# A four-part transformer block on one Trainium2 core: weight-block preparation placed behind each tile's last sum, priority for some sums, and one normalisation on ScalarE

## The chip, the cores and the metric

The kernel runs on one core of a Trainium2 chip. The metric is the device time of one execution in microseconds (us). The engines are TensorE (PE, with its weight loads shown apart as PEld), VectorE (DVE), ScalarE (ACT), GpSimd (POOL) and SyncE (SP, which issues nearly all of the DMAs here). Each engine works through its own instructions strictly in their order, and waits at the head of its queue for what that instruction needs.

## The reference, cut to what matters

The input is x, 4 batch entries of 512 tokens with 1024 channels each, in float32. Four layers follow one another, each with a layer norm (LN, no weights) ahead of it and a residual around it:

```python
x = x + attn0(LN(x))   # at each position: softmax attention among the 4 batch entries
x = x + ffn0(LN(x))    # h @ W_base.T + b_base + sum over 8 experts of
                       #   rw[e] * (h @ A[e].T) @ B[e].T, rank 16,
                       #   rw = softmax over the two largest of h @ W_gate.T, else 0
x = x + mla(LN(x))     # causal attention, 32 heads, low-rank q and kv, RoPE, output matrix wo
x = x + ffn1(LN(x))    # as ffn0, but rw[e] is one softmax over 8 experts for each batch entry,
                       #   from the mean of its tokens 179 to 510
```

## The kernel before, in words

The 2048 tokens are 16 tiles of 128 tokens, four tiles for each batch entry. A float32 product is done as three products of a reduced type: each operand is split into a high part (a cast, mostly on ACT) and a low part (operand minus high part, on DVE or POOL), and `matmul3` (L131 to L135) adds low x high, high x low and high x high in one PSUM bank. A scheduler lays out each engine's instructions from the program order, their dependencies and priorities. `tc.high_priority()` moves the instructions under it ahead where the data allow it. `tc.issue_after(ins)` puts the instructions under it behind `ins` in the order of an engine. It is an ordering of the schedule and adds no semaphore. Tiles of SBUF and PSUM come from pools with a fixed number of buffers, and a buffer that is taken again waits for its last reader.

**First feed-forward layer (about 107 to 380 us).** The loop over tiles stands at L465, with `s` the place of the tile in the order. The product of a tile has 1160 columns (gate, the experts' A, and base weights) in three parts of 392, 384 and 384, each in a PSUM bank. The pool `b_po` has six banks, so two tiles fit. For tile s, PE does in turn: part 0 of tile s+1; the transpose of tile s's weighted expert activations (`weigh`); part 1 of tile s+1; the transposes of the normalised tile s+2 (`turn0`); part 2 of tile s+1; and the product with the experts' B, into the banks of tile s (`finish`, L324). Then DVE adds each of the three banks to x (L333), which frees the bank; part 0 of tile s+2 needs the first one. Beside that DVE does the router's small steps (`route`), the normalisation (L124), and half of the splits. POOL adds the bias to x (L479). Every fourth tile the statistics of the next four tiles are taken (`statistics`, L119): those that the next layer needs at tiles 3, 7 and 11, and those of this layer at tiles 1, 5 and 9.

**Block preparation.** In the same loop, at tiles 2 to 9, `prepare_w1(room1, s - 2)` (L366 on) prepares eight blocks of weights for the last layer. That layer's matrix product is cut into two by two blocks and done with seven products instead of eight, some of which use differences of weight blocks. For each of the eight, DVE does four subtractions (L372, 128 x 288), ACT four copies (L375), POOL four subtractions (L376), and SP four writes to DRAM (L377, `w_t<-raw`). Then the next block is fetched (L363, `raw<-in_w_dram`). All of it lives in one room of SBUF, of which four parts hold the fetched block and three pairs of parts hold results, taken in turn (`n = 4 + 2 * ((4 * u + n) % 3)`). When the eight blocks are done, the room becomes `rawA`, into which the weights `waT` of the attention are loaded (L498 to L500). After each tile's sums SP writes the tile to DRAM (`x_d`, L492).

**Attention (about 380 to 1560 us).** It isn't touched, but for its end. `project(g, b, behind)` (L824) multiplies the context of a group of eight heads and one batch entry with the output matrix, in the same seven-product form: `b11, t1, t2, b22, t3, b21, t4`, into PSUM banks `poa` and `pob`. After each product DVE adds the bank to a piece `xs` of x (L877). ACT and POOL make the splits `cxh` and `cxl` (L838, L839) of the next operands.

**Transition (about 1555 to 1615 us).** The last `project`, of group NG-1 and batch NB-1, runs interleaved with the start of the second feed-forward layer: `norm(0, t)` (L1077) normalises the two tiles of the first pair from `xo[0]`, where x has been loaded, into `hs[0]`, by one DVE instruction each (L124); `turn1` (L1081) transposes them, four transposes to a PSUM bank, which ACT copies; `operands` (L1098) makes sums and differences s1, s2, s4 (L1103) and splits them. `split_w1` (L988) splits weight blocks `wb` on DVE or POOL.

**Second feed-forward layer (to the end).** Eight pairs of tiles, seven products each (`product`, L1221), for two column halves (`problems` holds the halves). After each, DVE adds the bank to `xo` (L1244). For the first pair the two halves are done one after the other, so there `problems` has one member; for all later pairs it has two.

Of the kernel before, what the change touches and what calls it, by code (L numbers as in the profile page):

```python
# [9 lines left out]
F32 = mybir.dt.float32  # L10
FR = mybir.dt.float32r
AF = mybir.ActivationFunctionType
ALU = mybir.AluOpType
# [4 lines left out]
P = 128  # L18
# [27 lines left out]
def block_kernel(ctx: ExitStack, tc: tile.TileContext, a: dict, out: bass.AP):  # L46
# [277 lines left out]
    def finish(xt, po, hw, cols, bt, to=None):  # L324

        at = 0
        first = cols[-1][1] - D
        for s, (c0, c1) in enumerate(cols):
            skip = first if s == 0 else 0
            n = c1 - c0 - skip  # L330
            matmul3(po[s][:, skip : c1 - c0], hw[0], hw[1], bt[0][:, at : at + n],
                    bt[1][:, at : at + n], start=False, stop=True, skip_group_check=True)
            V.tensor_tensor(xt[:, at : at + n], xt[:, at : at + n], po[s][:, skip : c1 - c0],  # L333
                            ALU.add)
            if to is not None:
                nc.sync.dma_start(out=to[:, at : at + n], in_=xt[:, at : at + n])
            at += n

    LAST = slice(2, 3)

# [25 lines left out]
    def prepare_w1(room, u):  # L366

        c, s = divmod(u, 2)
        b11, b12, b21, b22 = (room[:, k * W1B : (k + 1) * W1B] for k in range(4))
        for n, (kind, to, a0, a1) in enumerate((("t1", b11, b12, b11), ("t3", b12, b22, b12),  # L370
                                                ("t2", b22, b22, b11), ("t4", b21, b21, b22))):
            V.tensor_tensor(to, a0, a1, ALU.subtract)  # L372
            n = 4 + 2 * ((4 * u + n) % 3)
            h, l = (room[:, (n + k) * W1B : (n + k + 1) * W1B].bitcast(FR) for k in range(2))
            A.copy(h, to)  # L375
            G.tensor_tensor(l, to, f32(h), ALU.subtract)  # L376
            nc.sync.dma_start(  # L377
                out=w1_d[kind, s][:, :, c, :],
                in_=room[:, n * W1B : (n + 2) * W1B].rearrange("p (k n) -> p k n", k=2))
        if u + 1 < ND:  # L380
            fetch_w1(room, u + 1)
# [18 lines left out]
    with tc.tile_pool(name="b_h", bufs=2) as hp, tc.tile_pool(name="b_hTh", bufs=2) as hTh, \  # L400
            tc.tile_pool(name="b_hTl", bufs=2) as hTl, tc.tile_pool(name="b_w", bufs=1) as bwp, \
            tc.tile_pool(name="b_work", bufs=2) as wk, \
            tc.tile_pool(name="b_pt", bufs=2, space=PSUM) as ptp, \
            tc.tile_pool(name="b_po", bufs=6, space=PSUM) as pop:
        with tc.tile_pool(name="b_stB", bufs=1) as stage:
            b0h, b0l = load_split(bwp, stage, a["b0T"], [P, D], "b0", G)
        bias0 = broadcast_rows(bwp, a["b0"], D, "bias0")

        def route(lg):


            def best(values):
                m = small.tile([P, 1], F32, name="best")
                V.tensor_reduce(m, values, AX.X, ALU.max)
                eq = wk.tile([P, E], F32, name="eq")
                V.scalar_tensor_tensor(out=eq, in0=values, scalar=m, in1=rank,
                                       op0=ALU.is_equal, op1=ALU.mult)
                k = small.tile([P, 1], F32, name="key")
                V.tensor_reduce(k, eq, AX.X, ALU.max)
                one = wk.tile([P, E], F32, name="one")  # L420
                V.tensor_scalar(one, eq, k, None, ALU.is_equal)
                return m, one

            m1, one1 = best(lg)
            rest = wk.tile([P, E], F32, name="rest")
            V.scalar_tensor_tensor(out=rest, in0=one1, scalar=NEG, in1=lg, op0=ALU.mult, op1=ALU.add)
            m2, one2 = best(rest)
            e2 = small.tile([P, 1], F32, name="e2")
            V.tensor_tensor(e2, m2, m1, ALU.subtract)
            A.activation(e2, e2, AF.Exp)  # L430
            w1 = small.tile([P, 1], F32, name="w1")
            V.tensor_scalar(w1, e2, 1.0, None, ALU.add)
            V.reciprocal(w1, w1)
            w2 = small.tile([P, 1], F32, name="w2")
            V.tensor_tensor(w2, e2, w1, ALU.mult)
            rw = wk.tile([P, E], F32, name="rw")
            V.tensor_scalar(rw, one1, w1, None, ALU.mult)
            V.scalar_tensor_tensor(out=rw, in0=one2, scalar=w2, in1=rw, op0=ALU.mult, op1=ALU.add)
            return rw

        def routed(po):
            lg = wk.tile([P, E], F32, name="lg")
            V.tensor_copy(lg, po[0][:, ER : ER + E])
            return route(lg)

        def turn0(s):
            t = order[s]
            h = hp.tile([P, D], F32, name="h")
            with tc.high_priority() if s < 2 else ExitStack():
                normed.append(normalise(h, x[:, t, :], *stats0[s // NB], s % NB))  # L450
            return transposed(h, (hTh, hTl), ptp)

        normed = []
        hts = {0: turn0(0), 1: turn0(1)}
        po = {0: base(hts[0], w0, W0_COLS, pop, slice(0, 3))}
        room1 = raw()
        for kind in ("b11", "b22", "b21"):
            row, col = int(kind[1]) - 1, int(kind[2]) - 1
            for s in range(2):
                nc.sync.dma_start(  # L460
                    out=w1_d[kind, s][:, 0],
                    in_=a["w1"][row * ND // 2 : (row + 1) * ND // 2, :,
                                (2 * s + col) * W1B : (2 * s + col + 1) * W1B].rearrange("c p n -> p c n"))
        fetch_w1(room1, 0)
        for s, t in enumerate(order):  # L465
            if s + 1 < NT:
                po[s + 1] = base(hts[s + 1], w0, W0_COLS, pop, slice(0, 1))
            q, k = divmod(s, NB)
            hw = weigh(po[s], routed(po[s]), ptp, wk) if s + 1 < NT else hw_last
            if s + 1 < NT:  # L470
                po[s + 1] += base(hts[s + 1], w0, W0_COLS, pop, slice(1, 2))
            if k == 1 and q + 1 < TPB:
                with tc.issue_after(normed[1].ins):
                    stats0[q + 1] = statistics([x[:, n * TPB + q + 1, :] for n in range(NB)])
            if s + 2 < NT:
                hts[s + 2] = turn0(s + 2)
            if s == NT - 1:
                hts1[1] = turn1(1, ptp)
            G.tensor_tensor(x[:, t, :], x[:, t, :], bias0, ALU.add)  # L479
            if s == NT - 2:  # L480
                hw_last = weigh(po[s + 1], routed(po[s + 1]), ptp, wk)
            if s + 1 < NT:
                po[s + 1] += base(hts[s + 1], w0, W0_COLS, pop, LAST)
            if s == NT - 2:
                wpools.close()
                hTh1 = c1.enter_context(tc.tile_pool(name="c1_hTh", bufs=2, side="right"))
                hTl1 = c1.enter_context(tc.tile_pool(name="c1_hTl", bufs=2, side="right"))
                hp1 = c1.enter_context(tc.tile_pool(name="c1_h", bufs=2, side="right"))
                hts1[0] = turn1(0, ptp)
            finish(x[:, t, :], po.pop(s), hw, W0_COLS, (b0h, b0l))  # L490
            for k_ in range(2):
                nc.sync.dma_start(out=x_d[t][k_], in_=x[:, t, k_ * 512 : (k_ + 1) * 512])  # L492
            if k == NB - 1 and q < TPB - 1:
                stats1[q] = statistics([x[:, n * TPB + q, :] for n in range(NB)], "c", 4)
            if 0 <= s - 2 < ND:
                prepare_w1(room1, s - 2)
            if s == ND + 2:
                rawA = raw()  # L498
                for ch in range(ND):
                    nc.sync.dma_start(out=rawA[:, ch * NA : (ch + 1) * NA], in_=a["waT"][ch])  # L500
                split_shared(firstp, 0)
# [210 lines left out]
    with ExitStack() as c2:  # L712
# [111 lines left out]
        def project(g, b, behind):  # L824
# [17 lines left out]
            for j in range(0, TPB, 2):  # L842
# [16 lines left out]
                for kind, bank, start, to, last in (  # L859
# [11 lines left out]
                    for c, (wh, wl) in enumerate(w[kind]):  # L871
# [2 lines left out]
                                skip_group_check=True)  # L874
                        if c + 1 < HG // 4:
                            yield
                    V.tensor_tensor(xs[to], xs[to], banks[bank], ALU.add)  # L877
                    if last and (g, b) == (NG - 1, 0):
                        V.bn_stats(stats_d[j + to[0]][:, to[1], :], xs[to])
                    if last:  # L880
# [195 lines left out]

        def norm(q, t):  # L1077
            s = 2 * q + t
            normalise(hs[q][t], hs[q][t] if q else xo[0][t], *stats[s][0], stats[s][1])

        def turn1(q, half):  # L1081

# [138 lines left out]
    def product(q, step, problems):  # L1221
# [5 lines left out]
        for s in problems:  # L1227
# [13 lines left out]
                else:  # L1241
                    V.tensor_tensor(to, to, ps[:, 0:ER], ALU.add)
            to = xo[q][t][:, at : at + W1B - skip]
            V.tensor_tensor(to, to, ps[:, skip:W1B], ALU.add)  # L1244
            if kind == "t4" and q % 2:
                at = slice(0, 2 * W1B - ER) if s == 0 else slice(2 * W1B - ER, D)
                nc.sync.dma_start(out=out_v[:, 2 * q + 1, at], in_=xo[q][1][:, at])
# [124 lines left out]
```

## Time and profile before

| | us |
|---|---|
| median of the runs (3) | 1855.22 |
| lowest and highest | 1845.07 and 1857.25 |
| the profiled execution: its own time | 1851.48 |
| its span, first to last instruction | 1849.7 |
| mean TensorE clock granted in the span | 0.982 |

The profile is of one execution; the span lies within that execution's own time. The groups of the first feed-forward layer that matter here, as the profile gives them for the stretch from 107 to 380 us: the 48 sums L333 take 504 ns each (22.8 us); the 32 subtractions L372 take 688 ns each (22.0 us), and DVE stood idle for 12.2 us ahead of them, 11.2 of these for the DMA that fetches the block; the 32 copies L375 take 433 ns each on ACT, and the 32 subtractions L376 take 880 ns each on POOL; the 16 bias sums L479 take 2431 ns each on POOL; the 15 normalisations L124 take 975 ns each on DVE.

A group's line gives the line of code, the engine, the operation, output and input names with their shapes, the number of instructions, the busy time and mean duration, and then how long the engine had stood idle just before these instructions and what ended the idle time. Idle time costs something only on an engine that others wait for.

### The profile page before, as it was taken

The page shows a single profiled execution, that of the slowest core. Times are in us where ns is not written, and L with a number is a line of the kernel's source. Part 1 is how long each engine was busy: PE and PEld are TensorE (multiplying, and loading weights), DVE is VectorE, ACT ScalarE, POOL GpSimd, SP SyncE. Part 2 cuts the span into 40 slices and gives each one's busy share as a digit, 9 for nine tenths or more (in the row PEclk, how much of TensorE's full clock was granted, in tenths as well). Part 3 has the DMA queues.
Part 4 walks back from the last instruction along what each step waited for, and adds up shares of the span by engine and source line. Part 5 has one row for each costly group of instructions (what it writes and reads, how often), then busy time and mean ns, then how long its engine had stood idle before and what let it go on. Part 6 is the DMA issues. An engine that isn't in the chain of part 4 may idle for free.

```text
span 1849.7 us, 30780 instructions
## 1 busy us (share of the span) xinstructions
PE 1744.4 (94%) x10280; PEld 1463.2 (79%) x10280; DVE 1363.8 (74%) x3534; ACT 878.0 (47%) x2272; POOL 915.7 (50%) x819
## 2 busy tenths in 40 slices
PE   6978999999899999999999999999999999779998
PEld 6977899999667777767777767777766777679998
DVE  6787666576697777678777678777678877667785
ACT  6332211156675555466555465555466655323222
POOL 0364211020565566556566556566556665565552
PEclk9989899999899999999999999999999999989999
DMA  7235300035442333353243353242344233643431
GB/s 259 79 121 193 133 35 35 35 93 159 129 142 76 106 131 112 105 169 114 94 137 101 117 170 112 95 142 89 129 150 151 93 133 131 236 155 100 136 116 46
DMA packets 130239, 224.68 MB, mean 121 GB/s; under 512 B 22113, under 2 KB 57953, under 8 KB 127009
## 3 DMA queue, kind: packets, MB, share of 16 engines
q1 hardware_dynamic: 130080, 222.72, 35.9%
q8 instruction: 81, 1.33, 0.3%
q14 instruction: 78, 0.63, 0.1%
HBM read 155.55 MB, written 70.65 MB: 122 GB/s over the span
## 4 chain that ended last, share of the span: by engine, by line
PE 70%; DVE 10%; POOL 4%; ACT 3%; issue 2%; DMA 1%; SPq 0%; POOLq 0%; ACTq 0%; DVEq 0%
PE psv L817 8%; PE pst L801 6%; PE pss L133 3%; PE pss L134 3%; PE pss L135 3%; PE pob L133 3%; PE poa L133 3%; PE po L133 3%; PE po L134 3%; PE po L135 3%; PE psq L133 3%; PE acc L135 3%; PE acc L133 2%; PE pob L134 2%; PE psq L135 2%; PE pob L135 2%
## 5 line engine op out<-in xcount | busy, mean ns | idle before, releaser
L780 ACT ACTIVATE p<-p,mn 128x512 f32<-128x512 f32 (+3 forms) x512 | 284.3, 557 | 236.7 <-DVE mn L777 235.6
L602 POOL TENSOR_TENSOR qf<-qf,ropeT 64x512 f32<-64x512 f32 x128 | 167.7, 1311 | 220.8 <-ACT qf L598 217.1
L777 DVE CUSTOM_DVE_ANT_0 p<-pss,causal 128x512 f32<-128x512 f32 (+3 forms) x512 | 232.0, 487 | 24.8 <-PE pss L135 21.0
L801 PE MATMUL pst<-ident,p 128*128 128x128 f32 x1280 | 186.7, 276 | 5.6 <-ACT pT L803 4.7
L603 POOL TENSOR_TENSOR qf<-qf,t 64x512 f32<-64x512 f32 x128 | 165.6, 1294 | 46.6 <-DVE t L601 39.2
L801 PEld LDWEIGHTS pst<-ident,p 128*128 128x128 f32 x1280 | 154.8, 143 | 31.8 <-ACT pT L803 6.4
L803 ACT COPY pT<-pst 128x512 f32<-128x512 f32 x256 | 143.3, 578 | 58.2 <-PE pst L801 58.2
L133 PE MATMUL pss<-kT,ql 128*128 128x512 f32 (+2 forms) x384 | 144.4, 376 | 19.8 <-DVE mn L777 14.4
L611 POOL TENSOR_TENSOR ql<-qf,qh 128x384 fp32r<-128x384 f32 x128 | 131.3, 1026 | 58.6 <-DVE qh L610 58.6
L839 POOL TENSOR_TENSOR cxl<-s,cxh 128x256 fp32r<-128x256 f32 x128 | 96.7, 756 | 116.9 <-ACT cxh L838 111.6
L133 PE MATMUL po<-w_h,hTl 128*128 128x384 f32 (+1 forms) x384 | 136.0, 354 | 13.4 <-DVE x L333 13.4
L134 PE MATMUL po<-w_l,hTh 128*128 128x384 f32 (+1 forms) x384 | 132.9, 346 | 0.0
L135 PE MATMUL po<-w_h,hTh 128*128 128x384 f32 (+1 forms) x384 | 132.6, 345 | 0.0
L135 PE MATMUL pss<-kT,qh 128*128 128x512 f32 (+2 forms) x384 | 131.1, 341 | 0.0
L134 PE MATMUL pss<-kT,qh 128*128 128x512 f32 (+2 forms) x384 | 131.1, 341 | 0.0
L803 DVE COPY pT<-pst 128x256 f32<-128x256 f32 x128 | 53.8, 420 | 76.3 <-PE pst L801 75.0
L133 PEld LDWEIGHTS pss<-kT,ql 128*128 128x128 f32 x384 | 72.6, 189 | 46.5 <-DVE mn L777 22.8
L598 ACT COPY qf<-psq 128x512 f32<-128x512 f32 x126 | 73.6, 584 | 65.5 <-PE psq L135 65.3
L600 DVE TENSOR_TENSOR t<-psq,ropeT 32x512 f32<-32x512 f32 x126 | 87.7, 696 | 17.2 <-ACT qf L598 13.0
L780 ACT ACTIVATION_READ_ACCUMULATOR p<-p,mn 128x1 f32 x512 | 96.3, 188 | 0.0
L479 POOL TENSOR_TENSOR x<-x,bias 128x1024 f32<-128x1024 f32 x16 | 38.9, 2431 | 106.1 <-DVE h L124 82.3
L601 DVE TENSOR_TENSOR t<-psq,ropeT 32x512 f32<-32x512 f32 x126 | 87.1, 691 | 1.7
(548 smaller groups left out, 5082.4 us busy)
## 6 DMA issues: line engine op xcount, KB each, us to landing
xs<-x_d SPq DMA_DIRECT2D x128, 256.0 KB
x_d<-xs SPq DMA_DIRECT2D x128, 256.0 KB
slotC<-in_woT_dram SPq DMA_DIRECT2D x32, 512.0 KB
rb<-r_d SPq DMA_DIRECT2D x128, 128.0 KB
w_t<-raw SPq DMA_DIRECT2D x32, 288.0 KB
x<-in_x_dram SPq DMA_DIRECT2D x16, 512.0 KB
x_d<-x SPq DMA_DIRECT2D x32, 256.0 KB
slotA<-q_d SPq DMA_DIRECT2D x8, 1024.0 KB
```

The costliest lines, as they stand in the source:

```text
L133: T.matmul(ps, lhsT=al, rhs=bh, start=start, stop=False, **kw)
L134: T.matmul(ps, lhsT=ah, rhs=bl, start=False, stop=False, **kw)
L135: T.matmul(ps, lhsT=ah, rhs=bh, start=False, stop=stop, **kw)
L602: G.tensor_tensor(f[mid], f[mid], ropeT[mid, 0, :], ALU.mult)
L603: G.tensor_tensor(f[mid], f[mid], t2[mid], ALU.add)
L611: G.tensor_tensor(l, f[:, P:S], f32(h), ALU.subtract)
L777: V.tensor_tensor_reduce(out=to, in0=ps[:, 0:n], in1=causal[:, S - n : S], scale=1.0, scalar=-NEG, op0=ALU.add, op1=ALU.min, accum_out=mn[ ...
L780: A.activation(to, to, AF.Exp, bias=mn[:, i : i + 1], scale=-1.0, accum_out=rs[:, i : i + 1])
L801: T.transpose(ps[:, w : w + P], p[:, OF[i] + j * P : OF[i] + (j + 1) * P], ident)
L803: copy(pT[:, AT[js[0]] : AT[js[0]] + w], ps[:, 0:w])
L817: T.matmul(ps[n * KVR : (n + 1) * KVR, S - w : S], lhsT=k[:, j, :], rhs=pTs[u + n][:, AT[j] : AT[j] + w], start=(j == 0), stop=(j == TPB - 1))
L839: G.tensor_tensor(l, src, f32(h), ALU.subtract)
```

## The change

It has three parts. First, `finish` returns its last DVE instruction, and the block preparation is emitted under `tc.issue_after(done.ins)`: the DVE instructions of `prepare_w1` are ordered behind the last of the three sums of the tile at which they stand in the program. Second, two kinds of sums are emitted under `tc.high_priority()`: L877 in the last `project`, and L1244 where only one half is computed, that is for the first pair. Third, `norm(0, t)` is done on ACT, as `rstd * x + off`, with `off = -mean * rstd` from a new DVE instruction on 128 x 1; the later pairs stay on DVE.

```diff
@@ finish
-            V.tensor_tensor(xt[:, at : at + n], xt[:, at : at + n], po[s][:, skip : c1 - c0],
-                            ALU.add)
+            done = V.tensor_tensor(xt[:, at : at + n], xt[:, at : at + n],
+                                   po[s][:, skip : c1 - c0], ALU.add)
             if to is not None:
                 nc.sync.dma_start(out=to[:, at : at + n], in_=xt[:, at : at + n])
             at += n
+        return done
@@ the loop over tiles
-            finish(x[:, t, :], po.pop(s), hw, W0_COLS, (b0h, b0l))
+            done = finish(x[:, t, :], po.pop(s), hw, W0_COLS, (b0h, b0l))
             for k_ in range(2):
                 nc.sync.dma_start(out=x_d[t][k_], in_=x[:, t, k_ * 512 : (k_ + 1) * 512])
             if k == NB - 1 and q < TPB - 1:
                 stats1[q] = statistics([x[:, n * TPB + q, :] for n in range(NB)], "c", 4)
             if 0 <= s - 2 < ND:
-                prepare_w1(room1, s - 2)
+                with tc.issue_after(done.ins):
+                    prepare_w1(room1, s - 2)
@@ project
-                    V.tensor_tensor(xs[to], xs[to], banks[bank], ALU.add)
+                    with tc.high_priority() if (g, b) == (NG - 1, NB - 1) else ExitStack():
+                        V.tensor_tensor(xs[to], xs[to], banks[bank], ALU.add)
@@ norm
-            normalise(hs[q][t], hs[q][t] if q else xo[0][t], *stats[s][0], stats[s][1])
+            (mv, rstd), k = stats[s]
+            if q:
+                return normalise(hs[q][t], hs[q][t], mv, rstd, k)
+            off = small.tile([P, 1], F32, name="off")
+            V.scalar_tensor_tensor(out=off, in0=mv[:, k, 0:1], scalar=-1.0, in1=rstd[:, k : k + 1],
+                                   op0=ALU.mult, op1=ALU.mult)
+            A.activation(hs[0][t], xo[0][t], AF.Identity, bias=off, scale=rstd[:, k : k + 1])
@@ product
-            V.tensor_tensor(to, to, ps[:, skip:W1B], ALU.add)
+            with tc.high_priority() if len(problems) == 1 else ExitStack():
+                V.tensor_tensor(to, to, ps[:, skip:W1B], ALU.add)
```

## The prediction

> **What bounds the kernel now.** I read the page first, then the waits by engine, then the time order of single stages. TensorE carries the kernel, and where it stands still the time is lost.
>
> ```profile
> span 1849.7 us, 30780 instructions
> PE 1744.4 (94%) x10280; PEld 1463.2 (79%) x10280; DVE 1363.8 (74%) x3534; ACT 878.0 (47%) x2272; POOL 915.7 (50%) x819
> PE   6978999999899999999999999999999999779998
> PEclk9989899999899999999999999999999999989999
> ```
>
> Each digit is 46.2 us. Dips of PE stand where the change acts: slices 3 and 4 (139 to 231 us, the first feed-forward layer) and slices 34 and 35 (1572 to 1665 us, attention to second feed-forward layer). I asked for PE's waits in the two stages, 100 to 240 and 1560 to 1612 us:
>
> ```profile
> PE po L133 <- DVE x L333: 13.4, 4, 4.5
> ...
> PE pob L133 <- DVE xs L877: 5.3, 3, 2.4
> PE poa L133 <- POOL cxl L839: 1.2, 1, 1.2
> PE poa L133 <- DVE xs L877: 0.6, 1, 0.6
> ```
>
> Both times PE waits for a sum on DVE that frees a PSUM bank. Busy times by stretches, cut where the first-part products of tiles 2, 3, 4 ... start, show what one tile of the first layer costs (PE busy, PEld, DVE, ACT, POOL, then PE clock, DMA share, GB/s):
>
> ```profile
> 143.74:147.45 3.71, 0.00 (x1) 0.00 (x1) 3.61 (x6) 0.74 (x2) 3.71 (x3) 1.00 0.22 80
> 147.45:166.70 19.25, 16.86 (x91) 16.47 (x91) 14.03 (x36) 4.81 (x13) 9.11 (x10) 0.91 0.65 212
> 166.70:186.50 19.80, 15.30 (x91) 14.90 (x91) 13.91 (x35) 4.47 (x12) 8.62 (x9) 0.98 0.58 192
> 186.50:204.31 17.81, 17.81 (x91) 17.75 (x91) 11.47 (x33) 3.55 (x10) 7.51 (x8) 0.83 0.53 180
> 204.31:222.31 18.00, 15.19 (x91) 14.80 (x90) 14.79 (x48) 5.00 (x9) 3.54 (x3) 1.00 0.41 133
> 222.31:238.99 16.68, 16.68 (x90) 16.61 (x91) 8.20 (x28) 1.55 (x4) 2.40 (x1) 0.90 0.09 32
> 238.99:254.02 15.03, 15.03 (x91) 14.95 (x91) 8.07 (x28) 1.55 (x4) 2.40 (x1) 1.00 0.10 36
> 269.06:284.09 15.03, 15.03 (x91) 14.80 (x90) 14.63 (x47) 3.31 (x7) 2.40 (x1) 1.00 0.10 37
> ```
>
> A tile without block preparation takes 15.03 us, all PE. The stretch from 143.74 to 238.99 us is five tiles: 95.25 us against 75.15, an excess of 20.1 us. Of it 13.4 is standing and 6.7 is slow clock afterwards. The cause, in DVE's time order and on the chain that ended last:
>
> ```profile
> 144.47 2.59 DVE L372 TENSOR_TENSOR raw<-raw 128x288 f32<-128x288 f32 x2
> 174.59 0.46 DVE L372 TENSOR_TENSOR raw<-raw 128x288 f32<-128x288 f32 x1 [2.46 <-DMA raw<-in_w_dram]
> ...
> 169.99 5.20 DMA raw<-in_w_dram
> 181.00 3.57 DMA raw<-in_w_dram
> ```
>
> The 32 preparation subtractions (L372) stand in DVE's queue ahead of the tile sums, and some wait there for their DMA, with the sums behind them.
>
> **What the Trainium skill says.** "TensorE: Matmul & The Clock Gate", What's actually happening: PE falls to half clock after an idle window of about 3.4 us that runs freely, and needs about as long to recover. The trace agrees in kind: gaps of 3.71, 4.50 and 2.81 us were followed by 1.8, 2.8 and 1.65 us of loss, that of 2.39 us by 0.2. "SBUF — State Buffer", Who interferes with whom: a DVE instruction with two SBUF inputs and a GpSimd one that reads SBUF exclude each other for the whole instruction. The trace agrees: L435, a 128x1 product, took 2.19 us beside POOL's 2.40 us bias sum. "ScalarE: Activation LUTs", What ACT_TABLE_LOAD costs: an ACTIVATE is 186 ns, plus 93 ns for each pointer operand, plus 0.833 ns an element; by this estimate the new normalisation is 1.23 us. The trace shows a 128x1024 cast on ACT at 1.05 us.
>
> **Part 1, the ordering edge.** How the instructions stand in both builds shows that it takes hold: the 32 subtractions move from tiles 0 to 4 to behind the sums of tiles 2 to 9, four to a tile. PE's order in this stage is unchanged.
>
> Removed: the excess of 20.1 us, since no L372 is left ahead of the first two sums and the later ones start after their sum. At tile 0, DVE still has the logits, the next tile's normalisation and two splits, all without the DMA waits, so the sum at 143.1 us can follow its product at once.
>
> Added: four subtractions (0.43 to 0.69 us, the least and the mean of the 32) per tile, 1.7 to 2.75 us, and 4 x 0.81 us of POOL work that can block DVE. In a light tile DVE is busy for 8.07 of 15.03 us; it idles 2.31 us before the next logits, 1.53 before the normalisation and 2.52 before the sum. So six light tiles hide it: cost nothing; without that cover 2 us each.
>
> Two of the eight are heavy, tiles 3 and 7, where the next four tiles' statistics come too. There DVE is busy for 14.63 us and the bank is freed just in time (the next product starts 0.2 us late). Four subtractions lengthen it by 1.7 to 2.75 us plus up to 1 us of exclusion by POOL: a gap of 1.5 to 4, taken 2.7, and slow clock of 0.2 to 2.8, taken 1.3. Twice 4.0 is 8.0 us. Part 1: 20.1 - 8.0 = 12.1 us gained.
>
> Its DMAs: the fetch of the next block is issued after POOL's last split, some 6 us into the tile, takes 3.5 to 5.2 us, and is wanted at 15. On SP, the x_d writes now stand ahead of the w_t writes; nobody waits for either. The fourth ACT copy waits for the tile's first w_t write, since three room slots serve four blocks: subtraction 1.2, copy 1.7, POOL 2.55, issue 3.1, landing (2.47 us in the chain) 5.6 us after the product starts. Behind it on ACT stands the router's exponential, whose input comes at 6.4: no cost. The room is free later, about 290 us, so the waT load moves from 207 to 290; its parts are wanted at 372.
>
> **Part 2, priority, and part 3, ACT.** In the transition PE stands:
>
> ```profile
> 1577.09 0.47 PE L133 MATMUL pob<-t10h,cxl 128*128 128x512 f32 x1 [2.45 <-DVE xs L877]
> 1586.53 0.50 PE L133 MATMUL pob<-b220h,cxl 128*128 128x512 f32 x1 [2.09 <-DVE xs L877]
> 1588.82 0.47 PE L133 MATMUL poa<-t30h,cxl 128*128 128x512 f32 x1 [0.62 <-DVE xs L877]
> 1594.12 0.47 PE L133 MATMUL pob<-b110h,cxl 128*128 128x512 f32 x1 [0.79 <-DVE xs L877]
> 1597.10 0.47 PE L133 MATMUL poa<-t10h,cxl 128*128 128x512 f32 x1 [1.23 <-POOL cxl L839]
> ```
>
> That is 7.2 us, plus about 1.6 of slow clock (8 products at 0.43 instead of 0.23 us): 8.8. In the new order sums L877 precede the L1103 combinations and the L988 split, two 0.8 us normalisations leave DVE (two 0.15 us offsets come), and ten of the twelve b11 products of the next layer move behind, where they fill waits. What is late next: POOL's 3.2 us L988 split, now later because its ACT copy stands behind the two ACT normalisations, holds back the split of s1, so t10 starts near 1575.7 instead of 1577.1, 1.5 us after PE is free. Then about 0.5 at t20, 0.7 at b22, and near b21 up to 1.5 us, as DVE's next normalisation now stands behind h loads that are issued after the x_d writes. I take 3.5 us: gain 5.3, bounds 0 and 8. Later, at 1642 us, the s1 combination (2.86 us, blocked by POOL) now stands behind the router's small steps instead of ahead of them; PE stood 3.8 us there, I take 0.8 back (bounds -1 and 2). The chain b11, ah, al, s1, s2, s4, sum that costs 3.23 us at 1612.69 is untouched.
>
> **Sum.** 12.1 + 5.3 + 0.8 = 18.2 us. Profiled execution 1851.48 us (span 1849.7 and 1.8 around it), after: 1833.3. The median of the runs shown is 1855.22, 3.7 more: 1837.0.
>
> **The rivals.**
> - A, the heavy tiles don't stall: new order puts the small steps elsewhere and idle bits take the subtractions. For it: 0.4 us of DVE idle in tile 7; against: DVE at 96% there. Saves 18.5 in part 1 and 6.5 after: 1830.
> - B, the transition gives nothing, because POOL's L988 and the late h loads replace the sums as the last wait. For it: DMA share 0.95 at 1568 to 1577 us; against: 5.9 of 7.2 us wait for L877. Then 1855.2 - 9.2 = 1846.
> - C, slower: the fourth ACT copy waits for the w_t write and holds up exponential, router and sum in each of eight tiles. It decides once the landing takes over 7 us (0.8 us to the exponential, 4 us of DVE idle). Each such tile costs 3 us of standing and 1.7 of clock: 37.6 against 20.1 saved, less 6 in the transition: 1866. Against it: landings of 2.47 us in a DMA share of 0.5, and the share falls to about 0.25.
> - That the edge does nothing is excluded by the order.
>
> **How the numbers follow.** Forecast 0.50 (own range 1832 to 1842), A 0.26, B 0.19, C 0.05. The range of 1826 to 1849 takes in A, B and the bounds. A measurement can tell about 1% of this kernel, 18.6 us, from no change: faster by over 1% is below 1836.7, that is A and two fifths of the forecast, 0.46; within 1% is the rest of the forecast, B and half of C, 0.51; slower 0.03.
>
> **What would show it.** Right: no PE wait on x L333 before the sum of tile 3, tiles of 15.0 us, and two waits of 1.5 to 4 us near tiles 4 and 8; PE waits on xs L877 nearly gone at 1555 to 1590 us. Wrong: PE waiting on L333 in every prepared tile (C), ACT copies of L375 waiting long for w_t, or sums in the transition standing behind a normalisation that waits for its h load (B).

## The result, and the profile after

The changed kernel takes 1836.47 us (median of 11 runs, 1834.84 to 1840.72) against 1849.08 us for the kernel before (median of 11 runs, 1845.06 to 1857.25). The ratio is 0.9933, 95% interval 0.9916 to 0.995: 0.67% or 12.4 us faster, with bounds of 9 and 16 us. The three runs shown ahead of the prediction had a median of 1855.22 us; with eight more the median came out 6 us lower.

The page of the kernel after, the lines that answer to those shown of before:

```profile
span 1834.7 us, 30780 instructions
PE 1741.2 (95%) x10280; PEld 1461.5 (80%) x10280; DVE 1350.6 (74%) x3534; ACT 880.0 (48%) x2274; POOL 917.0 (50%) x819
PE   6979999999899999999999999999999999879998
PEclk9989999999999999999999999999999999989999
```

The dip of slices 3 and 4 is gone, that of slices 34 and 35 is smaller. PE does the same work (1741.2 against 1744.4 us), and the span is 15.0 us shorter. The waits of PE from 100 to 300 us, one line of the answer (sum, times, longest):

```profile
PE po L133 <- DVE x L333: 4.3, 2, 2.1
```

Four waits of 13.4 us became two of 4.3. The stretches, cut at the first products of tiles 4, 5, 6, 7 and 9, 10, 11 (PE, PEld, DVE, ACT, POOL busy, PE clock, DMA share, GB/s):

```profile
173.64:188.74 15.10, 15.10 (x91) 15.02 (x91) 10.27 (x32) 3.28 (x8) 6.26 (x5) 1.00 0.47 153
188.74:206.14 17.40, 15.26 (x91) 14.86 (x90) 17.19 (x52) 6.12 (x12) 6.08 (x5) 1.00 0.39 133
206.14:221.35 15.21, 15.21 (x91) 15.14 (x92) 10.40 (x32) 3.28 (x8) 6.21 (x5) 1.00 0.47 152
251.55:268.95 17.40, 15.26 (x91) 14.86 (x91) 17.19 (x52) 6.12 (x12) 6.08 (x5) 1.00 0.39 133
268.95:285.68 16.73, 16.73 (x90) 16.66 (x91) 10.40 (x32) 3.17 (x8) 6.19 (x5) 0.90 0.42 138
```

A tile with a preparation and no statistics (the first row) costs PE nothing: DVE has 10.27 us of work in 15.10. In the two stretches that hold a preparation and the statistics DVE has 17.19 us of work and the next tile's bank comes 2.14 us late: the late sums are those of tiles 4 and 8, and PE stands ahead of the first products of tiles 6 and 10. Inside the first of them, from DVE's and POOL's order of time:

```profile
193.74 0.95 DVE L373 TENSOR_TENSOR raw<-raw 128x288 f32<-128x288 f32 x1
202.65 2.37 POOL L480 TENSOR_TENSOR x<-x,bias 128x1024 f32<-128x1024 f32 x1 [5.94 <-DVE w L433]
202.87 2.17 DVE L436 TENSOR_TENSOR w<-e,w 128x1 f32<-128x1 f32 x1
205.68 1.34 DVE L333 TENSOR_TENSOR x<-x,po 128x256 f32<-128x256 f32 x3
```

A product of 128x1 took 2.17 us beside a bias sum on POOL; elsewhere it takes 0.16 (that the bias sum is the reason is shown by e9 below). The sums start only after it, with no idle time ahead of them.

The transition, from PE's order of time, the products ahead of which PE stood:

```profile
1563.53 0.50 PE L133 MATMUL pob<-t10h,cxl 128*128 128x512 f32 x1 [0.82 <-POOL cxl L841]
1565.74 0.47 PE L133 MATMUL poa<-t20h,cxl 128*128 128x512 f32 x1 [0.56 <-DVE xs L880]
1568.64 0.47 PE L133 MATMUL pob<-b220h,cxl 128*128 128x512 f32 x1 [0.24 <-DVE xs L880]
1581.61 0.47 PE L133 MATMUL poa<-b220h,cxl 128*128 128x512 f32 x1 [1.64 <-DVE xs L880]
```

Five gaps of 7.2 us became four of 3.3. Of the 7.2 us some 1.3 vary from execution to execution: in e7 and e12 below, where PE, DVE and ACT have the order of the kernel before, the gaps make 5.8 and 5.9 us. Where the 15.0 us of span went can be read by setting each product of one trace against the same product of the other: at the end of the first feed-forward layer the kernel after is 13.4 us ahead, at 1550 us 11.7, behind the last projection 17.8, and from 1660 us on 15.8 to 15.2. So the transition gave 6.1 us with its slow clock, and about 2.2 were lost again at once.

### The profile page after: what moved, and what is told of

It is laid out like the page before. It is cut to its first block, busy times and chain, and to the rows that moved or that the text cites. A ratio compares the mean times of both kernels' runs of the same rounds, so it can differ in the third digit from the quotient of the medians.

```text
span 1834.7 us, 30780 instructions
## 1 busy us (share of the span) xinstructions
PE 1741.2 (95%) x10280; PEld 1461.5 (80%) x10280; DVE 1350.6 (74%) x3534; ACT 880.0 (48%) x2274; POOL 917.0 (50%) x819
## 4 chain that ended last, share of the span: by engine, by line
PE 78%; DVE 10%; POOL 4%; ACT 3%; issue 2%; DMA 1%; SPq 0%; POOLq 0%; ACTq 0%; DVEq 0%
PE psv L819 8%; PE pst L803 6%; PE pss L133 4%; PE po L133 4%; PE po L135 4%; PE po L134 4%; PE pss L134 3%; PE pss L135 3%; PE pob L133 3%; PE poa L133 3%; PE psq L133 3%; PE psq L134 3%; PE psq L135 3%; PE pob L135 3%; PE pob L134 3%; PE acc L135 3%
## 5 line engine op out<-in xcount | busy, mean ns | idle before, releaser
L880 DVE TENSOR_TENSOR xs<-xs,pob 128x512 f32<-128x512 f32 x112 | 76.0, 679 | 15.2 <-PE pob L135 13.5
```

## The experiments

**Each part by itself.** e1 is the kernel before with the edge, e2 with the two priorities, e3 with the normalisation on ACT; each edit is the part of the diff shown above.

> The kernel before with the ordering edge alone. Theory (the gain is DVE's order in the first feed-forward layer): tile starts as in the changed kernel, PE stands for x L333 only twice, about 2.1 us each, ahead of tiles 6 and 10; the last sum of this layer ends about 13.4 us earlier; the transition keeps its five gaps of 7.2 us in all. Time about 13 us below before, ratio 0.993. Rival (most of the gain is made in the transition): ratio 0.996 or above. The changed kernel measured 0.9933, so by the theory nearly all of it is here.

Measured: ratio 0.9929 (0.9908 to 0.995), two PE gaps of 2.19 and 2.21 us ahead of tiles 6 and 10. The last products of the first layer start 16.4 us earlier, 2.0 of which were there before this layer began; the transition has four gaps of 5.95 us, not five of 7.2. The first-layer gain is all there, and with it the whole gain of the change.

> The kernel before with the two priorities alone. The order of instructions shows only two sums moved (the sum at t1 of the second pair of tiles ahead of two operand combinations, and the first sum of the next layer ahead of one); no sum of L1244 after that one moves. Theory (the priority does little): PE gaps on xs L877 fall from 5.9 us to 4 to 6 us, time within 2 us of before, ratio 0.999 to 1.000. Rival (the priority is what shortens the transition): gaps on xs L877 of 1 us or less, 4 to 5 us gained, ratio 0.9975.

Measured: ratio 1.0001 (0.9987 to 1.0016). PE's waits from 1540 to 1610 us:

```profile
PE pob L133 <- DVE xs L878: 4.6, 2, 2.5
PE poa L133 <- DVE xs L878: 1.1, 1, 1.1
```

The waits on the sums are still 5.7 us of 5.9. A priority moves a sum only where the scheduler had something else ahead that could wait; there were two such places.

> The kernel before with the first pair normalised on ACT alone. In the order of instructions this part carries nearly all that moves in the transition and at the mixture. Theory: PE gaps between the last projection's products fall from 7.2 to about 3.4 us, as in the changed kernel, and the wait of PE for the first weighed activations rises from 1.75 to about 3.2 us; together 2 to 4 us gained, ratio 0.998. Rival (the normalisation on ACT costs what it saves): ratio 1.000 or above.

Measured: ratio 0.9999 (0.9986 to 1.0012). The gaps of the transition are those of the changed kernel:

```profile
PE poa L133 <- DVE xs L877: 2.2, 2, 1.6
PE pob L133 <- POOL cxl L839: 0.8, 1, 0.8
PE pob L133 <- DVE xs L877: 0.2, 1, 0.2
```

So the normalisation on ACT, not the priority, made the transition shorter, by 6.1 us in this trace too; and yet the kernel is no faster. Something takes the gain back. One thing was visible in all traces with this part: a light tile of the first layer, more than 1000 us ahead of the changed code, took 15.10 us instead of 15.03 to 15.05.

**The heavy tiles.** e4 is the changed kernel with no preparation where the statistics are:

```diff
+    PREPARE = (1, 2, 4, 5, 6, 8, 9, 10)
...
-            if 0 <= s - 2 < ND:
+            if s in PREPARE:
                 with tc.issue_after(done.ins):
-                    prepare_w1(room1, s - 2)
-            if s == ND + 2:
+                    prepare_w1(room1, PREPARE.index(s))
+            if s == PREPARE[-1] + 1:
```

> The changed kernel, with the eight preparations at tiles 1, 2, 4, 5, 6, 8, 9 and 10 instead of 2 to 9, so none at tiles 3 and 7, and waT loaded one tile later. Theory (four subtractions too many on a DVE that is full in the tiles with statistics): no PE gap above 0.3 us at tiles 2 to 12, all periods about 15.1 us, 4.6 us of standing and up to 1.6 us of slow clock gone against the changed kernel: ratio to before 0.990. Rival (the stall comes from elsewhere in these tiles, for instance the bias sum of POOL that blocks L436 for 2 us): gaps of about 2 us stay and the ratio is 0.993.

Measured: ratio 0.9897 (0.9878 to 0.9916), and no wait on L333 from 120 to 350 us. The stretch of tile 5 in e4:

```profile
190.45:205.65 15.20, 15.20 (x91) 14.86 (x90) 14.86 (x48) 3.31 (x7) 2.41 (x1) 1.00 0.09 35
```

DVE works 14.86 of 15.20 us, and that is just enough, although the 128x1 product still takes 2.21 us there. The other load in these stretches is the bias sum that blocks L436. e6 emits POOL's bias sums of tiles 3 and 7 ahead of `turn0`:

```diff
+            if s in (3, 7):
+                G.tensor_tensor(x[:, t, :], x[:, t, :], bias0, ALU.add)
             if s + 2 < NT:
                 hts[s + 2] = turn0(s + 2)
-            G.tensor_tensor(x[:, t, :], x[:, t, :], bias0, ALU.add)
+            if s not in (3, 7):
+                G.tensor_tensor(x[:, t, :], x[:, t, :], bias0, ALU.add)
```

> The changed kernel, with POOL's bias sum of tiles 3 and 7 emitted ahead of the normalisation of tile s+2, so that it no longer runs beside L436. DVE's order is unchanged. Theory (two things fill DVE in the heavy tiles, the four subtractions and the 2.0 us for which POOL's bias sum blocks L436, and either is enough to close the gap of 2.14 us): L436 takes 0.2 us, the gaps ahead of tiles 6 and 10 fall to below 0.5 us, 4 us gained against the changed kernel, ratio to before 0.991. Rival (the bias sum then blocks other instructions of DVE with two operands in SBUF, above all the subtractions, for as long): gaps of 1.5 us or more stay, ratio 0.993.

Measured: ratio 0.9933 (0.9912 to 0.9953), L436 still 2.17 us, gaps 2.14 and 2.15 us. The edit moved nothing: in the trace every engine has the sequence of operations of the changed kernel, POOL's included. So this run says nothing for or against the bias sum. POOL runs ahead of PE, and the bias sums in the heavy stretches are those of tiles 8 and 12. e9 orders these two behind POOL's splits of a later preparation:

```diff
-            G.tensor_tensor(x[:, t, :], x[:, t, :], bias0, ALU.add)
+            with tc.issue_after(split[s - 6]) if s in (8, 12) else ExitStack():
+                G.tensor_tensor(x[:, t, :], x[:, t, :], bias0, ALU.add)
...
-            G.tensor_tensor(l, to, f32(h), ALU.subtract)
+            split[u] = G.tensor_tensor(l, to, f32(h), ALU.subtract).ins
```

> The changed kernel, with POOL's bias sums of tiles 8 and 12 ordered behind the preparation that follows, which takes them out of the two stretches with statistics (the run before aimed at tiles 3 and 7, whose bias sums do not stand there: POOL runs up to four tiles ahead). DVE's order is unchanged. Theory (in the two heavy stretches DVE is late by the four subtractions and by 2.0 us for which a bias sum blocks L436; the first product there is late by 2.14 us): L436 takes 0.2 us there, the gaps ahead of tiles 6 and 10 fall from 2.14 us to 0.1 to 0.5 us, with the slow clock 4 to 6 us are gained, ratio to before 0.9905. Rival (the subtractions and POOL's splits beside them are the whole of the delay, and DVE idles elsewhere for what it gains): gaps of 1.5 us or more, ratio 0.993.

Measured: ratio 0.9883 (0.9865 to 0.99), a larger gain than expected. Set product against product, the trace of e9 gains 5.5 us on that of the changed kernel in this stage, as expected; the rest arose where the order is the same, and is not explained. The orders of PE, DVE and ACT are those of the changed kernel. The 128x1 product in its order of time, and PE's waits from 120 to 350 us:

```profile
200.87 0.16 DVE L438 TENSOR_TENSOR w<-e,w 128x1 f32<-128x1 f32 x1
```

```profile
PE po L133 <- DVE x L333: 0.2, 1, 0.2
```

The gaps fell from 2.14 to 0.16 and 0.15 us. Two causes added up, and to remove either is enough: e4 took away the subtractions and left the blocked product, e9 the reverse.

**What made the sums late before.** e5 leaves out the fetches of blocks 1 to 7:

```diff
-        if u + 1 < ND:
-            fetch_w1(room, u + 1)
```

> The kernel before without the fetches of the blocks 1 to 7: the eight preparations are done one after the other on what lies in the room, so the last layer's weight differences are other numbers, and seven fetches are left out. The subtractions stand even further ahead in DVE's order. Theory (the sums were late because they stood behind subtractions that waited for their block): the excess of tiles 1 to 6 over 15.03 us falls from 23.9 us to between 5 and 12 us, what is left being the subtractions' own time; ratio 0.992 to 0.995. Rival (the mere work of the preparation on DVE in these tiles, or exclusion by POOL, made the delay): the excess stays above 17 us, ratio 0.997 or above.

The 23.9 us in this expectation counts the first gap twice; tiles 1 to 6 of before take 110.5 us, 20.3 more than six of 15.03. Measured: ratio 0.9976 (0.9964 to 0.9987), an excess of 13.8 us: the excess lies between the two theories, the ratio in the rival's range. PE's waits from 120 to 350 us and the group of the subtractions from 100 to 260 us (busy, mean ns, idle before, what ended it):

```profile
PE po L133 <- DVE x L333: 9.9, 2, 6.9
```

```profile
L372 DVE TENSOR_TENSOR raw<-raw 128x288 f32<-128x288 f32 x32 | 20.3, 640 | 5.9 <-POOL raw L376 4.9 <-DVE raw L372 0.5
```

Without the fetches one third of the loss goes. Two thirds stay: the sums still stand behind the subtractions, which now wait for POOL's splits in the same room. This is no exact division of the loss before, since the subtractions also stand further ahead in DVE's order here. It shows that a fetch which costs no wait would not be enough; the order is what e1 shows to be the cure.

**The place of the operands.** The new 128x1 tile `off` has three buffers and takes 96 bytes of each partition ahead of most other tiles. e7 is the kernel before with nothing but such a tile:

```diff
+    G.memset(small.tile([P, 1], F32, name="pad", bufs=3), 0.0)
```

> The kernel before with nothing but a tile of 128x1 more in the pool of small tiles, three buffers, set once to zero at the start. It takes 96 bytes of each partition, as the tile off of the changed kernel does, and moves most tiles behind it from a multiple of 64 bytes to 32 beyond one; DVE, ACT, PE and SP have the same instructions in the same order. Theory (all three kernels with the normalisation on ACT ran every product about 0.6 ns longer, 15.10 us a tile instead of 15.03 to 15.05, because of where their operands lie): light tiles of 15.10 us and 3 to 6 us more in all, ratio 1.002 to 1.003. Rival (the longer products come from something else, or by chance of the run): tiles of 15.03 to 15.05 us, ratio 1.000.

Measured: ratio 1.0012 (1.0001 to 1.0023), 2.2 us slower, less than expected, and the interval nearly reaches 1. e8 is e4 with the offset kept in a tile that is there already, `name="nmx1"` instead of `name="off"`:

> The changed kernel with the preparations away from tiles 3 and 7 (at 1, 2, 4, 5, 6, 8, 9, 10), and the offset of the ACT normalisation kept in a small tile that exists already (the one of nmx1), so that no tile moves against the kernel before. Theory of the place of the operands: light tiles of 15.03 to 15.05 us, 3 to 6 us less than with the preparations away alone, ratio to before 0.987. Rival (no effect of the place): tiles of 15.10 us, ratio 0.990.

Measured: ratio 0.9883 (0.9863 to 0.9903), against 0.9897 for e4; in medians 1827.68 against 1831.85 us; the two intervals overlap. e12 is e7 with `bufs=2`:

> The kernel before with the same unused 128x1 tile, but two buffers of it: the tiles behind it move by 64 bytes of each partition, not by 96, so each keeps its place against a multiple of 64. The order of instructions is that of before but for the one fill. Theory (products are longer where operands lie 32 bytes beyond a multiple of 64): light tiles of 15.03 to 15.05 us, products of the query projection start to start about 227 ns as before and not 231.5 ns, ratio 1.000. Rival (any displacement, or one more tile, makes the products longer): 15.10 us and 231.5 ns, ratio 1.001 or above.

Measured: ratio 1.0001 (0.9992 to 1.001). One tile without preparation in e7 and in e12, and one of e8 with a preparation that is hidden beside it:

```profile
314.43:329.53 15.10, 15.10 (x91) 15.02 (x91) 8.09 (x28) 2.83 (x5) 2.40 (x1) 1.00 0.09 35
```

```profile
310.84:325.90 15.06, 15.06 (x91) 14.99 (x91) 8.08 (x28) 2.83 (x5) 2.40 (x1) 1.00 0.09 35
```

```profile
296.23:311.26 15.03, 15.03 (x91) 14.96 (x91) 10.24 (x32) 5.07 (x10) 7.18 (x6) 1.00 0.58 195
```

That the shift by 96 bytes makes PE's products longer is shown: PE has the same instructions in the same order in before and e7, and keeping the tiles in place (e8) brings 15.03 us back. What it costs the whole kernel is less sure: about 2 us, by intervals that nearly reach 1 or overlap. The rule of the 64 bytes is not: at a shift of 64 the tile takes 15.07 us from start to start, in between. The products of the query projection (`psq`), start to start in the trace (mean of the values between the tenth and the seventieth percentile), took 228.6 ns before, 231.5 in e7 and still 230.5 in e12, while those of 384 columns with kT took 175.9, 177.1 and 175.4. On which address bits it depends stays open.

**The mixture.** Behind the transition PE waits for the first weighed activations: 1.75 us before, 3.18 after. DVE and POOL in the changed kernel:

```profile
1624.42 0.17 DVE L1199 RECIPROCAL rden<-den 128x1 f32<-128x1 f32 x1 [0.46 <-ACT ex L1197]
1626.03 2.85 DVE L1112 TENSOR_TENSOR s<-a,a 128x512 f32<-128x512 f32 x1 [1.45 <-POOL al L1119]
1628.81 1.22 DVE L1201 TENSOR_SCALAR rw<-ex,rden 128x8 f32<-128x8 f32 x1
```

```profile
1622.38 2.38 POOL L1222 TENSOR_TENSOR raw<-raw,bias 128x1024 f32<-128x1024 f32 x1 [0.19 <-DVE raw L1254]
1624.72 1.28 POOL L1119 TENSOR_TENSOR al<-s,ah 128x512 fp32r<-128x512 f32 x1
1625.96 2.37 POOL L1222 TENSOR_TENSOR xo<-xo,bias 128x1024 f32<-128x1024 f32 x1
```

A bias sum now runs on POOL ahead of the split for which s1 waits, a second one blocks s1 until 1628.8, and the mixture's last step, rw, stands behind s1. e10 is e8 with the bias sums of the first two pairs emitted later:

```diff
-            if step == 5 and more:
+            if step == 5 and more and q:
                 biased(q + 1)
+            if step == 0 and q == 1:
+                biased(0)
+                biased(1)
             if step == 6 and q == 0:
-                biased(0)
```

> The changed kernel with the preparations away from tiles 3 and 7 and the offset in an existing tile, and besides with POOL's bias sums of the first two pairs of the second feed-forward layer emitted after the first product of the second pair; in POOL's order one bias sum moves behind the split of an operand. Theory (the first weighed activations come 1.4 us later with the ACT normalisation because a bias sum of 2.4 us on POOL blocks the combination s1 on DVE, and the mixture's last step stands behind it): the wait of PE ahead of the transposed weighed activations falls from 3.2 to about 1.7 us, ratio to before 0.9875. Rival (the next bias sum or the split blocks DVE for as long): wait of 3 us or more, ratio 0.988.

Measured: ratio 0.9858 (0.9841 to 0.9874), the fastest version of all at 1825.28 us. Its interval overlaps that of e8; set product against product, its trace gains 3.0 us on e8's at this place. s1 takes 1.76 us and PE's wait falls further than expected:

```profile
1617.71 1.76 DVE L1113 TENSOR_TENSOR s<-a,a 128x512 f32<-128x512 f32 x1 [1.47 <-POOL al L1120]
```

```profile
1620.28 0.30 PE L318 MATMUL pt<-ident,hw 128*128 128x128 f32 x1 [1.11 <-issue]
```

e11 is edge, priorities and e4's places without the normalisation on ACT:

> Edge, priorities and the preparations away from tiles 3 and 7, without the normalisation on ACT: the first pair is normalised on DVE as before, and no tile moves. Theory (the ACT normalisation is worth 3 to 5 us once it does not move the other tiles): light tiles of 15.03 to 15.05 us, the transition's gaps back at about 7 us, ratio to before 0.990 to 0.991. Rival (the ACT normalisation gives nothing even so): ratio 0.988.

Measured: ratio 0.9906 (0.9892 to 0.992), light tiles of 15.03 to 15.05 us, three gaps of 5.7 us in the transition (7 were expected). Against e8 (0.9883) the normalisation on ACT is worth 0.0023 of the time, 4 us, when it moves no tile. The two intervals overlap a little; product against product, the trace of e8 ends 3.8 us ahead.

## Why the prediction was right, and where not

**Part 1, right in place and size.** The excess of 20.1 us fell to two heavy tiles, named ahead, with gaps of 2.14 us (2.7 was taken). Slow clock of 1.3 us was taken for each; one had 1.6, the other none (its next tile, at full clock, took 15.20 us, as the tile in this place takes in e4 without a gap). The gain of 12.1 us came out as 13.4 in the trace, and as 13.1 in the times of e1 (0.0071 of 1850.94). The delay in the heavy tiles held both terms of the prediction, four subtractions and exclusion by POOL; the larger piece of exclusion, though, was the one that was there before, L436 beside the bias sum, as e9 shows. Rival A had DVE's idle bits take the subtractions; they didn't. Rival C is in the trace and harmless: in tile 2 the fourth copy starts 1.4 us after its subtraction, at 179.13 us, when the exponential has nothing to do yet. The subtractions waited for no DMA at all.

**The cause of the loss before was told in part.** The prediction had the sums behind subtractions of which some wait for their DMA. That wait is in the trace, but without those DMAs two thirds of the excess remain (e5): standing behind subtractions delays the sums with the fetches or without. The cure, which is the order, was right.

**The transition, right in size, wrong in who does it.** 3.5 us of gaps were to stay, 3.3 did, and the 1.6 us of slow clock went; gain in the trace 6.1 us for 5.3. The waits on the sums were to be nearly gone; 2.4 us of 5.9 stayed. Three gaps stood where they were expected (0.82 for 1.5, 0.56 for 0.5, 0.24 for 0.7). The fourth was to be a wait behind late h loads and was one of 1.64 us behind three combinations L1112, which took 0.99, 1.67 and 1.21 us beside POOL's splits instead of 0.68. The priority, which the prediction credited together with the normalisation, does nothing measurable (e2). The two new ACT normalisations took 1.24 and 1.25 us; 1.23 had been estimated.

**The mixture, wrong sign.** The step "the s1 combination now stands behind the router's small steps instead of ahead of them; I take 0.8 back" looked at lg, nmx and rden only. The last one, rw, had stayed behind s1, and s1 itself had become later through POOL's order. In place of 0.8 us won, 2.2 were lost by the trace, outside the bounds of -1 and 2; e10 gets back 4.6 us of the kernel's time (0.0025, from e8), more than was lost, though with overlapping intervals; by the traces it is 3.0.

**Not seen at all: the tile `off`.** It was costed as two instructions of 0.15 us. By its room alone it costs 2.2 us (e7), or 2.6 by the ratios of e4 and e8. With this and the mixture, parts 2 and 3 together gave nothing where 6.1 us were forecast: the edge alone has the ratio 0.9929, the whole change 0.9933. That is the outcome of rival B, though not for its reasons.

**The sum.** 18.2 us were forecast, 12.4 measured: part 1 gave one more, the transition about one more, the mixture three less, the displaced tiles two to three less. That makes 14.6, near the 15.0 by which the two profiled executions differ; the rest lies within the spread of single executions. The median after, 1836.47 us, lies at the forecast of 1837.0 by luck: the kernel before turned out 6 us faster than the three runs shown, and the gain was forecast by half too high.

## What to carry to other kernels

Work that is wanted late and is scheduled early belongs behind the instruction that frees the bottleneck's buffer; look then for the stretches where that engine is full and keep the work out of them, or take away what blocks it there. A 128x1 product that takes two microseconds can be a sign of another engine's long instruction beside it. When a new tile is added, look at a stretch far from the change: if the same products got longer there, the tile may have moved their operands, and a tile that exists already may hold the value.

## What the runs showed of the hardware

- Operands moved by 96 bytes in each partition made a tile of 91 PE instructions 15.10 us instead of 15.03, at a granted clock of 1.00 in both.
- A DVE product of 128x1 took 2.17 us beside a POOL sum of 2.37 us, and 0.16 us once that sum ran elsewhere (e9).
- A PE gap of 2.14 to 2.21 us is sometimes followed by half clock and sometimes not: of the six such gaps in the changed kernel, e1 and e6, four lost 1.6 us in the next tile and two 0.1. The traces' records of the granted clock show what decides. In each of the 14 traces every change of the clock lies on one grid with steps of 3.41 us. These are stretches of the changed kernel cut along its grid, with the columns as above:

```profile
201.79:205.20 3.41, 2.21 (x14) 1.89 (x12) 3.31 (x5) 0.00 (x0) 2.37 (x1) 1.00 0.00 0
205.20:208.61 3.41, 2.47 (x14) 2.47 (x15) 3.37 (x9) 0.62 (x2) 0.64 (x1) 1.00 0.36 133
266.64:270.05 3.41, 1.27 (x7) 1.10 (x7) 3.34 (x8) 0.00 (x0) 1.18 (x1) 1.00 0.00 0
270.05:273.46 3.41, 3.41 (x13) 3.41 (x12) 3.06 (x7) 1.30 (x3) 2.68 (x3) 0.50 0.54 197
```

  The gap that ends at 206.14 us is divided by a boundary into 1.20 and 0.94 us, and no half clock follows. The one that ends at 268.95 us lies whole in one stretch, and the next stretch runs at half clock. The other four gaps fit this. Of the stretches at full clock in all 14 traces, none of the 7012 in which PE stood for less than 1.5 us is followed by half clock, 49 of the 83 with 1.5 to 1.96 us are, and all 104 with more. The Trainium skill ("TensorE: Matmul & The Clock Gate", What's actually happening) has the activity counted in windows of 3413 ns that run freely, which agrees. Its idle window of about 3.4 us, on which the prediction drew, doesn't: here about half of one was enough.
- Later in the kernel a gap of 1.80 us at 1045 us cost 1.5 us of slow clock before, and one of 1.78 us at the same product cost none after. Both lay whole in one stretch of the grid, in the range where both happen. Single traces drift apart by such amounts where the code is the same: those of e2 and before, which differ only in the transition, were 2.5 us apart ahead of it.
